# Moving x loads and output stores to ScalarE's queue, and finishing the last units chunk by chunk, in a four-layer graph network kernel

## The chip, the cores and the metric

The kernel runs on one core of one Trainium2 chip. The metric is device time in microseconds (us) of that core. A core has TensorE (PE; PEld is its weight load), VectorE (DVE), ScalarE (ACT), GpSimd (POOL) and SyncE (SP), each with its own instruction queue, worked off in order; they wait for each other by semaphores. DMAs are issued from SP's or ScalarE's queue ("SPq", "ACTq" in the profile) and then run by themselves. Instructions are known in the profile by the line of the kernel that issued them (L876).

## The reference, cut to what matters

x is 64 graphs of 256 nodes with 128 features; adj is one 256x256 adjacency matrix for all. Four layers follow each other, each `x = layernorm(x + layer(x))`, all in fp32:

```python
def _layernorm(x, axis=-1, eps=1e-5):
    m = jnp.mean(x, axis=axis, keepdims=True)
    v = jnp.var(x, axis=axis, keepdims=True)
    return (x - m) / jnp.sqrt(v + eps)

# layer 0: attention whose logits are sums over pairs of nodes, in an index pattern that depends on n alone
h = x @ others_weight
u1 = h @ att_weight[:f_out, 0]; u2 = h @ att_weight[f_out:, 0]
e = u1[:, idx1] + u2[:, idx2]
e = jnp.where(e >= 0, e, 0.1 * e)
att = softmax(jnp.where(adj > 0, e, NEG_BIG), axis=1)
out = jnp.einsum('bik,bkl->bil', att, h) + x @ self_weight
# layer 1: graph attention: softmax over leaky_relu(e_src + e_dst), masked by adj + I, then elu(attn @ (x @ W))
# layer 2: five steps of a gated recurrence: m = adj @ h; z, r = sigmoid(...); hv = tanh(...); h = (1-z)h + z hv
# layer 3: x W0 + sum over k = 1..3 of adj^k x (Wk + Wk+3)
```

## The kernel before, in words

Two graphs make a unit (UB = 2), so there are 32 units (NU) of 512 rows. Ten units are in flight, each in a lane (LANES) with its own SBUF buffers: unit u lives in lane u % 10, and when it ends, unit u + 10 starts there. The buffer `m` of a lane receives a unit's x from DRAM, and is used again for products later; `x` holds the unit's current features, and the output is stored from it.

The kernel does not issue instructions as it goes. Functions `layer0` to `layer3` record tasks with `add(engine, ns, fn, reads, writes)`: an engine, an estimated duration, a closure and the cells that it reads and writes. `Plan.run` then walks a simulated clock: for each engine that is free it takes the ready task with the lowest key. The key (`first`) is the unit's number times PERIOD plus the task's due time, which is reached by adding up estimated durations along the unit's own dependencies, times PACE (PACE_GATED in layer 2). The order in which tasks are taken is the order of each engine's instructions; semaphores are placed by dependency. A DMA recorded for SP occupies that queue for its estimate (540 ns for a load of x), and counts as landed 4 us later. PSUM has eight banks, taken by tasks when they start.

Names and lines that matter here:
- `load_x` (L301): for the first XDIRECT = 9 units, one DMA brings x with rows on partitions, and TensorE turns it (`feature_major`, L524, four transposes). For later units, four DMAs (L309) bring 32x32 blocks, and VectorE turns them (L626).
- Row sums in layer 0: for units from DIRECT_ROWS = 4 on, a vector `cu` is stored to DRAM (`to_row`, L551) and read back in another layout, both spread over all partitions (`from_row`, L555) and as 64x15 pieces (L655), which a small add (L658) sums to `d`. For units 0 to 3, TensorE spreads it by transposing a broadcast column (L567) and makes `d` by four 128x1 products (L664).
- Layer 1 (L735): units below HALVES = 2 go through attention graph by graph (two halves), others in one piece: Prelu (L741), Exp (L744), the multiply by the mask (L745), products with x (L752) and with W (L764).
- `warm` (L346): matmuls whose results nobody uses. Four stand at the start; six are recorded with the rank of a unit after the last, so that they are taken when TensorE has nothing else to do.
- Layer 2: `far(u, step)` says whether the features are turned by way of DRAM (L916, L919, L922) or on TensorE (L941). Each step has six 128x512 products on TensorE (L876), three tanh on ScalarE (L887, L895, L904) and four elementwise rows on VectorE.
- Layer 3: products with the weights (L977), copies (L981), products with adj squared (L984) into two banks, one for each chunk c of 128 nodes, then `layernorm` with the statistics (L578), `ve` (L580), `rstd` by pow on GpSimd (L583), the shift (L589, L591) and the normalized rows (L604 on ScalarE or L612 on VectorE).
- The output: for units below 29, one store on SP (L989). The last three units store each chunk by itself on SP (L993), chunk 0 normalized on VectorE and chunk 1 on ScalarE.

```python
        return (t.unit if t.unit < NU - LANES else NU - 1 - LATE - (NU - 1 - t.unit) * TAIL) * PERIOD + t.due
```

The functions that the diff touches, with the line numbers of the profile:

Of the kernel before, what the change touches and what calls it, by code (L numbers as in the profile page):

```python
# [9 lines left out]
AF = mybir.ActivationFunctionType  # L10
# [13 lines left out]
SCALES = True  # L24
SMALL = ("ve", "cu", "d", "elu", "shift")
TIGHT = 4
HALVES = 2
FIRST_FAR = {0: 2, 1: 2}
LAST_FAR = {0: 1}
PERIOD = 43e3  # L30
TAIL = 0.3
LATE = 6
PACE = 2.8
PACE_GATED = 1.56
HOLD = 80
DIRECT_ROWS = 4
XDIRECT = 9
START = 35e3
R2 = 1
R3 = 1.5  # L40
# [158 lines left out]
def kernel(  # L199
# [45 lines left out]
    def cell(name, shape):  # L245
        return Cell(sb(name, shape))
# [54 lines left out]
    def load_x(u, by="sp"):  # L301
        z = lanes[u % LANES]["m"]
        if u < XDIRECT:
            queue = {"sp": nc.sync, ACT: nc.scalar}[by]
            add(by, 600, lambda: queue.dma_start(z.ap.rearrange("p (b c d) -> p b c d", b=UB, c=NC), x_u[u]), (), (z,), dma=True, wait=800)
            return
        parts = object()
        for a in range(D // BL):
            add("sp", 540, lambda a=a: nc.sync.dma_start(  # L309
                z.ap[a * BL : (a + 1) * BL].rearrange("j (b i) -> j b i", i=BL),  # L310
                x_a[u, a].rearrange("(b j) i -> j b i", j=BL)), (), (z,), group=parts)

    w1 = load("w1", W, [D, D])
    load_x(0, ACT)
# [27 lines left out]
    def warm(n, after=()):  # L342

        for _ in range(n):
            ps = bank()
            add(PE, mm_ns(N), lambda ps=ps: nc.tensor.matmul(  # L346
                ps.ap[:, 0:N].rearrange("p (k n) -> p k n", k=2), ident.ap,
                ident.ap.rearrange("p (o n) -> p o n", o=1).to_broadcast([P, 2, P]), start=True, stop=True), (ident,), (ps,), after)
# [219 lines left out]
                ps.ap[:, g * P : (g + 1) * P], view()[:, g : g + 1].to_broadcast([P, P]), ident.ap), (src, ident), (ps,))  # L568
        return ps, lambda: ps.ap.rearrange("q (b c p) -> q b c p", b=UB, c=NC)

    def layernorm(u, L, pairs, swap=False, centred=False, last=False):

        st, ve, rstd, nm = L["st"], L["ve"], L["rstd"], L["nm"]
        sts, xs = object(), object()
        for k, (c, view) in enumerate(pairs):
            add(DVE, 330, lambda k=k, view=view: nc.vector.bn_stats(st.ap[:, k, :], view().rearrange("p j d -> p d j")),  # L578
                (c,), (st,), group=sts)
        small(u, "ve", 150, lambda eng: eng.tensor_scalar(  # L580
            ve.ap.rearrange("p (k j) -> p k j", k=2), st.ap.rearrange("p k (j s) -> p k j s", j=2)[:, :, :, 2], 1.0 / D, EPS,
            op0=ALU.mult, op1=ALU.add), (st,), (ve,))
        add(POOL, 1050, lambda: nc.gpsimd.tensor_tensor(rstd.ap, ve.ap, nhalf.ap, op=ALU.pow), (ve, nhalf), (rstd,))  # L583
        by_act = u >= TIGHT and plan.layer in NORM

        if by_act and not centred:
            mean = st.ap.rearrange("p k (j s) -> p k j s", j=2)[:, :, :, 1]
            if "shift" in SMALL:
                add(POOL, 280, lambda: nc.gpsimd.tensor_scalar_mul(  # L589
                    nm.ap.rearrange("p (k j) -> p k j", k=2), mean, -1.0), (st,), (nm,))  # L590
                add(POOL, 250, lambda: nc.gpsimd.tensor_mul(ve.ap, nm.ap, rstd.ap), (nm, rstd), (ve,))  # L591
            else:
                add(DVE, 120, lambda: nc.vector.scalar_tensor_tensor(
                    ve.ap.rearrange("p (k j) -> p k j", k=2), mean, -1.0,
                    rstd.ap.rearrange("p (k j) -> p k j", k=2), op0=ALU.mult, op1=ALU.mult), (st, rstd), (ve,))
        for k, (c, view) in enumerate(pairs):

            act = by_act and (k or not last)
            for j in range(2):
                b, ch = (j, k) if swap else (k, j)  # L600
                at = slice(2 * k + j, 2 * k + j + 1)
                shift, col = (ones, slice(0, 1)) if centred else (ve, at)
                if act:
                    add(ACT, 400, lambda j=j, b=b, ch=ch, view=view, at=at, shift=shift, col=col: nc.scalar.activation(  # L604
                        X[u].ap[:, b, ch, :], view()[:, j, :], AF.Identity, bias=shift.ap[:, col], scale=rstd.ap[:, at]),
                        (c, shift, rstd), (X[u],), group=xs)
                elif centred:
                    add(DVE, 260, lambda j=j, b=b, ch=ch, view=view, at=at: nc.vector.tensor_scalar(
                        X[u].ap[:, b, ch, :], view()[:, j, :], rstd.ap[:, at], 1.0, op0=ALU.mult, op1=ALU.add),
                        (c, rstd), (X[u],), group=xs)  # L610
                else:
                    add(DVE, 260, lambda k=k, j=j, b=b, ch=ch, view=view, at=at: nc.vector.tensor_scalar(  # L612
                        X[u].ap[:, b, ch, :], view()[:, j, :], st.ap[:, k, 3 * j + 1 : 3 * j + 2], rstd.ap[:, at],
                        op0=ALU.subtract, op1=ALU.mult), (c, st, rstd), (X[u],), group=xs)

    def y_pairs(y):
        v = y.ap.rearrange("p (b c d) -> p b c d", b=UB, c=NC)
# [3 lines left out]
    def layer0(u, L):  # L621
# [24 lines left out]
        small(u, "lrelu", 100, lambda eng: eng.scalar_tensor_tensor(  # L646
            cu.ap[:, 2], cu.ap[:, 2], 0.1, cu.ap[:, 2], op0=ALU.mult, op1=ALU.max), (cu,), (cu,))
        row, rv = on_all(u, lc, L["row"], cu, lambda: cu.ap[:, 2])
        if u >= DIRECT_ROWS:
            to_row(L["rowu"], cu, lambda: cu.ap[:, 0:2].rearrange("p k g -> p (k g)"), 2 * G)  # L650


            parts = object()
            for c in range(NC):
                add("sp", 560, lambda c=c: nc.sync.dma_start(  # L655
                    u4.ap[c * P // 2 : (c + 1) * P // 2],
                    L["rowu"].ap[:, c : c + 2 * T].rearrange("o (i n) -> (o i) n", n=16)[:, 0:15]), (L["rowu"],), (u4,), group=parts)
            small(u, "d", 100, lambda eng: eng.tensor_add(d.ap, u4.ap[:, 0:3:2], u4.ap[:, 12:15:2]), (u4,), (d,))  # L658
            ds = d
        else:  # L660
            ds = bank()
            for b in range(UB):
                for k in range(2):
                    add(PE, 240, lambda b=b, k=k: nc.tensor.matmul(  # L664
                        ds.ap[:, b : b + 1], xb[:, b, k : N : 2], wx0.ap[:, D + 2 + k : D + 3 + k],
                        start=(k == 0), stop=(k == 1)), (xT, wx0), (ds,))
# [61 lines left out]
    def layer1(u, L):  # L728
# [47 lines left out]
                        (ps_o, rs), (hp,), group=parts)  # L776
        if not u:
            plan.rank = NU
            warm(6, [plan.tasks[-1]])
            plan.rank = None  # L780

        sign = -1.0 if "elu" in SMALL and u >= TIGHT else 1.0
# [173 lines left out]
    def layer3(u, L):  # L956
        xT = turned(u, L, STEPS)
        aT, s = L["m"], L["z"]
        if STEPS in FAST and far(u, STEPS):
            left_fast(X[u], lambda g: X[u].ap.rearrange("p b c d -> p (b c) d")[:, g], adjf, L["r"], L["z"], aT)  # L960
            tail = [t for t in plan.tasks[-4:-3]]
        else:
            ps_a = bank()
            for b in range(UB):
                left(ps_a, X[u], b)
            add(ACT, 500, lambda: nc.scalar.copy(aT.ap, ps_a.ap), (ps_a,), (aT,))
            tail = list(ps_a.writers)

        ps = [bank() for _ in range(NC)]

        def view(c):
            return ps[c].ap.rearrange("p (k b d) -> p k b d", k=2, b=UB)

        for k, src in enumerate((xT, aT)):
            for c in range(NC):
                for b in range(UB):
                    add(PE, mm_ns(N), lambda k=k, src=src, c=c, b=b: nc.tensor.matmul(  # L977
                        view(c)[:, :, b, :], bn(src.ap)[:, b, c * P : (c + 1) * P], w3.ap[:, k],
                        start=(k == 0 and b == 0), stop=(k == 1), skip_group_check=True), (src, w3), (ps[c],), tail)
        for c in range(NC):  # L980
            add(ACT, 300, lambda c=c: nc.scalar.copy(s.ap[:, c * N : (c + 1) * N], ps[c].ap[:, N : 2 * N]), (ps[c],), (s,), group=ps)  # L981
        for c in range(NC):
            for mc in range(NC):
                add(PE, mm_ns(N), lambda c=c, mc=mc: nc.tensor.matmul(  # L984
                    ps[c].ap[:, 0:N], a2T.ap[:, mc, c * P : (c + 1) * P], s.ap[:, mc * N : (mc + 1) * N],
                    start=False, stop=(mc == NC - 1), skip_group_check=True), (a2T, s), (ps[c],))
        layernorm(u, L, [(ps[c], lambda c=c: view(c)[:, 0]) for c in range(NC)], swap=True, last=u >= NU - 3)
        if u < NU - 3:
            add("sp", 450, lambda: nc.sync.dma_start(out_u[u], X[u].ap), (X[u],), ())  # L989
            return  # L990

        for c, done in enumerate((plan.tasks[-4:-2], plan.tasks[-2:])):
            add("sp", 450, lambda c=c: nc.sync.dma_start(out_u[u][:, :, c], X[u].ap[:, :, c]), (), (), done)  # L993

    def spawn(u, lane):
        for k, layer in enumerate((layer0, layer1, layer2, layer3)):
# [47 lines left out]
```

The softmax here doesn't subtract the row's maximum and nothing guards it: scores larger than these inputs give would overflow.

## Time and profile before

| | |
|---|---|
| three runs, median (lowest to highest) | 1395.87 us (1395.82 to 1396.42) |
| span of the profiled execution | 1395.9 us, clock 0.999 |
| DVE busy | 1207.8 us, 2880 instructions |
| ACT busy | 936.3 us, 2155 instructions |
| POOL busy | 258.6 us, 492 instructions |
| DMA | 146.52 MB, 16 engines 46.7% busy for queue q1 (SP's), 0.1% for q10 (ScalarE's) |
| x loads and output stores on SP | 100 and 35 issues |

Busy time is the sum of the records of an engine; issuing a DMA is not counted in it. Records of matmuls overlap each other, and the page says that their ends are modelled. The slices divide the span into 40 equal parts; a digit is the busy share in tenths, and PEclk is the clock that TensorE was granted. A line of the waits reads: engine, what it was to write, its line, what it waited for, then total us, times, longest us. A line of a chain reads: start, us, engine, what is written, line.

### The profile page before, as it was taken

The page shows a single profiled execution, that of the slowest core. Times are in us where ns is not written, and L with a number is a line of the kernel's source. Part 1 is how long each engine was busy: PE and PEld are TensorE (multiplying, and loading weights), DVE is VectorE, ACT ScalarE, POOL GpSimd, SP SyncE. Part 2 cuts the span into 40 slices and gives each one's busy share as a digit, 9 for nine tenths or more (in the row PEclk, how much of TensorE's full clock was granted, in tenths as well). Part 3 has the DMA queues.
Part 4 walks back from the last instruction along what each step waited for, and adds up shares of the span by engine and source line. Part 5 has one row for each costly group of instructions (what it writes and reads, how often), then busy time and mean ns, then how long its engine had stood idle before and what let it go on. Part 6 is the DMA issues. An engine that isn't in the chain of part 4 may idle for free.

```text
span 1395.9 us, 21958 instructions
## 1 busy us (share of the span) xinstructions
PE 1387.0 (99%) x6549; PEld 965.9 (69%) x6549; DVE 1207.8 (87%) x2880; ACT 936.3 (67%) x2155; POOL 258.6 (19%) x492
## 2 busy tenths in 40 slices
PE   9999999999999999999999999999999999999998
PEld 8766666676666776676766767777666656666776
DVE  7898998998889888888899798899888998898953
ACT  5897754556676677667677688897765545665443
POOL 3211110021122112122111122132011100112222
PEclk9999999999999999999999999999999999999999
DMA  4223545365364555555554555545463453445521
GB/s 118 41 54 84 123 100 112 90 131 120 91 134 107 110 119 102 121 113 111 112 115 106 119 120 105 119 107 119 105 132 93 105 116 87 114 103 113 126 56 46
DMA packets 530791, 146.52 MB, mean 105 GB/s; under 512 B 457968, under 2 KB 496112, under 8 KB 530672
## 3 DMA queue, kind: packets, MB, share of 16 engines
q1 hardware_dynamic: 529872, 144.59, 46.7%
q8 instruction: 53, 0.87, 0.3%
q14 instruction: 66, 0.54, 0.2%
q10 hardware_dynamic: 800, 0.52, 0.1%
HBM read 80.57 MB, written 64.45 MB: 104 GB/s over the span
## 4 chain that ended last, share of the span: by engine, by line
PE 98%; DVE 1%; POOL 0%; ACT 0%; issue 0%; ACTq 0%; DVEq 0%; POOLq 0%
PE ps L876 49%; PE ps L819 17%; PE ps L977 8%; PE ps L802 5%; PE ps L715 4%; PE ps L984 4%; PE ps L752 4%; PE ps L764 2%; PE ps L710 2%; PE ps L639 2%; PE ps L346 0%; PE ps L524 0%; POOL rstd L583 0%; PE ps L941 0%; DVE st L578 0%; PE ps L567 0%
## 5 line engine op out<-in xcount | busy, mean ns | idle before, releaser
L876 PE MATMUL ps<-m,gT 128*128 128x512 f32 x960 | 464.3, 592 | 0.0
L876 PEld LDWEIGHTS ps<-m,gT 128*128 128x128 f32 x960 | 171.5, 190 | 119.9 <-issue 97.7
L895 ACT ACTIVATE e<-ps,bias 128x512 f32<-128x512 f32 x160 | 109.9, 687 | 120.2 <-PE ps L876 115.2
L887 ACT ACTIVATE e<-ps,bias 128x512 f32<-128x512 f32 x160 | 110.0, 687 | 91.7 <-PE ps L876 91.1
L583 POOL TENSOR_TENSOR rstd<-ve,nhalf 128x4 f32<-128x4 f32 x128 | 147.8, 1155 | 110.5 <-DVE ve L580 76.4
L876 PE MATMUL ps<-e,u5T 128*128 128x512 f32 x320 | 163.1, 592 | 0.0
L580 POOL TENSOR_SCALAR ve<-st 128x4 f32<-128x4 f32 x112 | 34.9, 311 | 691.1 <-DVE st L578 613.1
L819 PEld LDWEIGHTS ps<-adjTf,ht 128*128 128x128 f32 x726 | 115.7, 191 | 67.5 <-issue 57.1
L904 ACT ACTIVATE p<-ps,bias 128x512 f32<-128x512 f32 x160 | 109.6, 685 | 49.7 <-PE ps L876 45.9
L819 PE MATMUL ps<-adjTf,e 128*128 128x128 f32 x968 | 137.7, 275 | 0.0
L819 PEld LDWEIGHTS ps<-adjTf,e 128*128 128x128 f32 x968 | 125.2, 192 | 13.4 <-issue 12.4
L819 PE MATMUL ps<-adjTf,ht 128*128 128x128 f32 x726 | 122.4, 274 | 0.0
L906 DVE SCALAR_TENSOR_TENSOR p<-e,p 128x512 f32<-128x512 f32 x160 | 109.1, 683 | 11.1 <-ACT p L904 10.1
L876 PEld LDWEIGHTS ps<-e,u5T 128*128 128x128 f32 x320 | 59.9, 190 | 61.0 <-issue 46.8
L876 PE MATMUL ps<-xT,gT 128*128 128x512 f32 x192 | 96.7, 593 | 0.0
L846 DVE TENSOR_TENSOR m<-ps,e 128x256 f32<-128x256 f32 x152 | 63.0, 417 | 34.5 <-PE ps L819 28.9
L741 ACT ACTIVATE e<-m,esd 128x256 f32<-128x256 f32 x112 | 80.8, 765 | 0.0
L890 DVE SCALAR_TENSOR_TENSOR e<-e,xT 128x512 f32<-128x512 f32 x96 | 65.3, 680 | 13.6 <-ACT e L887 12.2
L537 DVE STREAM_TRANSPOSE p<-x 128x512 f32<-128x512 f32 x61 | 67.1, 1102 | 8.5 <-ACT x L604 7.4
L578 DVE BATCH_NORM_STATS2 st<-ps 128x6 f32<-128x256 f32 x128 | 51.5, 420 | 25.6 <-PE ps L984 18.2
L715 PEld LDWEIGHTS ps<-ht,p 128*128 128x128 f32 x512 | 66.0, 190 | 9.1 <-issue 7.9
L849 DVE TENSOR_TENSOR m<-ps,m 128x256 f32<-128x256 f32 x152 | 62.5, 415 | 9.5 <-PE ps L819 8.6
(187 smaller groups left out, 2864.4 us busy)
## 6 DMA issues: line engine op xcount, KB each, us to landing
hb<-p SPq DMA_DIRECT2D x182, 256.0 KB, 2.1
ht<-hb SPq DMA_DIRECT2D x484, 64.0 KB, 2.5
xT<-hb SPq DMA_DIRECT2D x244, 64.0 KB, 2.6
m<-row SPq DMA_DIRECT2D x56, 256.0 KB, 3.9
hb<-p SPq DMA_DIRECT2D x124, 64.0 KB, 1.8
ht<-hb SPq DMA_DIRECT2D x31, 256.0 KB, 3.0
out_dram<-x SPq DMA_DIRECT2D x29, 256.0 KB, 2.8
m<-in_x_dram SPq DMA_DIRECT2D x92, 64.0 KB, 2.3
```

Source lines behind the costliest of these rows:

```text
L537: add(DVE, 1050, lambda: nc.vector.transpose(v.ap.rearrange("p (a g i) -> p g a i", g=G, i=BL), X[u].ap.rearrange("p b c (j a) -> p (b c) ...
L583: add(POOL, 1050, lambda: nc.gpsimd.tensor_tensor(rstd.ap, ve.ap, nhalf.ap, op=ALU.pow), (ve, nhalf), (rstd,))
L715: add(PE, mm_ns(D + 2), lambda b=b, ic=ic, kc=kc, yv=yv: nc.tensor.matmul(yv()[:, ic, :], p.ap[:, b * NC + kc, ic * P : (ic + 1) * P], h.a ...
L741: add(ACT, 600, lambda g=g, b=b: nc.scalar.activation(e.ap[:, g, :].rearrange("p (c n) -> p c n", c=NC), ev()[:, b], AF.Prelu, bias=esd.ap ...
L802: add(PE, mm_ns(N), lambda b=b, mc=mc: nc.tensor.matmul(ps.ap[:, b * N : (b + 1) * N], lhs(b, mc), mat.ap[:, mc, :], start=(mc == 0), stop ...
L819: add(PE, mm_ns(P) + 4, lambda: nc.tensor.matmul(ps.ap[:, at * P : (at + 1) * P], lhs(), mat.ap[:, k, c * P : (c + 1) * P], start=True, st ...
L876: add(PE, mm_ns(T), lambda: nc.tensor.matmul(ps.ap, w(), rhs.ap, start=start, stop=stop, skip_group_check=True), (c, rhs), (ps,), after)
L887: add(ACT, 600, lambda ps_g=ps_g, up=up: nc.scalar.activation(r.ap, ps_g.ap, AF.Tanh, bias=bias2.ap[:, 1:2], scale=0.5 / up), (ps_g, bias2 ...
L895: add(ACT, 600, lambda ps_g=ps_g, up=up: nc.scalar.activation(z.ap, ps_g.ap, AF.Tanh, bias=bias2.ap[:, 0:1], scale=0.5 / up), (ps_g, bias2 ...
L904: add(ACT, 600, lambda ps_v=ps_v, up=up: nc.scalar.activation(v.ap, ps_v.ap, AF.Tanh, bias=bias2.ap[:, 2:3], scale=1 / up), (ps_v, bias2), ...
L906: add(DVE, 600, lambda: nc.vector.scalar_tensor_tensor(v.ap, z.ap, 1.0, v.ap, op0=ALU.add, op1=ALU.mult), (v, z), (v,))
L977: add(PE, mm_ns(N), lambda k=k, src=src, c=c, b=b: nc.tensor.matmul(view(c)[:, :, b, :], bn(src.ap)[:, b, c * P : (c + 1) * P], w3.ap[:, k ...
```

## The change

x loads from unit 10 on, and the output stores but those of the last two units, are recorded for ScalarE and issued from its queue. The last two units go through a new `layernorm_last`: each chunk has its own statistics, `ve` (on VectorE), pow (on GpSimd, 128x2 instead of 128x4) and shift (on VectorE); graph 1's rows of each chunk are normalized on ScalarE, graph 0's on VectorE, and each chunk is stored by SP as soon as its two rows are done. Unit 29 takes the ordinary way. The fourth unit (u = 3) makes its `d` by way of DRAM (DIRECT_D = 3), while its row is still spread by TensorE. XDIRECT goes from 9 to 10, so that unit 9's x is loaded by one DMA and turned by TensorE. HALVES goes from 2 to 0: no unit goes graph by graph through layer 1. PACE goes from 2.8 to 3.0.

```diff
--- before.py
+++ after.py
@@ -24,17 +24,19 @@
 SCALES = True
 SMALL = ("ve", "cu", "d", "elu", "shift")
 TIGHT = 4
-HALVES = 2
+HALVES = 0
+DIRECT_D = 3
+WARM = 6
 FIRST_FAR = {0: 2, 1: 2}
 LAST_FAR = {0: 1}
 PERIOD = 43e3
 TAIL = 0.3
 LATE = 6
-PACE = 2.8
+PACE = 3.0
 PACE_GATED = 1.56
 HOLD = 80
 DIRECT_ROWS = 4
-XDIRECT = 9
+XDIRECT = 10
 START = 35e3
 R2 = 1
 R3 = 1.5
@@ -306,9 +308,9 @@
             return
         parts = object()
         for a in range(D // BL):
-            add("sp", 540, lambda a=a: nc.sync.dma_start(
+            add(ACT, 540, lambda a=a: nc.scalar.dma_start(
                 z.ap[a * BL : (a + 1) * BL].rearrange("j (b i) -> j b i", i=BL),
-                x_a[u, a].rearrange("(b j) i -> j b i", j=BL)), (), (z,), group=parts)
+                x_a[u, a].rearrange("(b j) i -> j b i", j=BL)), (), (z,), group=parts, dma=True)
 
     w1 = load("w1", W, [D, D])
     load_x(0, ACT)
@@ -568,7 +570,7 @@
                 ps.ap[:, g * P : (g + 1) * P], view()[:, g : g + 1].to_broadcast([P, P]), ident.ap), (src, ident), (ps,))
         return ps, lambda: ps.ap.rearrange("q (b c p) -> q b c p", b=UB, c=NC)
 
-    def layernorm(u, L, pairs, swap=False, centred=False, last=False):
+    def layernorm(u, L, pairs, swap=False, centred=False):
 
 
 
@@ -594,13 +596,11 @@
                     ve.ap.rearrange("p (k j) -> p k j", k=2), mean, -1.0,
                     rstd.ap.rearrange("p (k j) -> p k j", k=2), op0=ALU.mult, op1=ALU.mult), (st, rstd), (ve,))
         for k, (c, view) in enumerate(pairs):
-
-            act = by_act and (k or not last)
             for j in range(2):
                 b, ch = (j, k) if swap else (k, j)
                 at = slice(2 * k + j, 2 * k + j + 1)
                 shift, col = (ones, slice(0, 1)) if centred else (ve, at)
-                if act:
+                if by_act:
                     add(ACT, 400, lambda j=j, b=b, ch=ch, view=view, at=at, shift=shift, col=col: nc.scalar.activation(
                         X[u].ap[:, b, ch, :], view()[:, j, :], AF.Identity, bias=shift.ap[:, col], scale=rstd.ap[:, at]),
                         (c, shift, rstd), (X[u],), group=xs)
@@ -612,6 +612,27 @@
                     add(DVE, 260, lambda k=k, j=j, b=b, ch=ch, view=view, at=at: nc.vector.tensor_scalar(
                         X[u].ap[:, b, ch, :], view()[:, j, :], st.ap[:, k, 3 * j + 1 : 3 * j + 2], rstd.ap[:, at],
                         op0=ALU.subtract, op1=ALU.mult), (c, st, rstd), (X[u],), group=xs)
+
+    def layernorm_last(u, pairs):
+
+        xs = object()
+        for k, (c, view) in enumerate(pairs):
+            st, ve, rstd = (cell(f"{name}{k}_{u}", [P, n]) for name, n in (("st", 6), ("ve", 2), ("rstd", 2)))
+            mean, var = (st.ap.rearrange("p (j s) -> p j s", j=2)[:, :, s] for s in (1, 2))
+            add(DVE, 330, lambda view=view, st=st: nc.vector.bn_stats(st.ap, view().rearrange("p j d -> p d j")), (c,), (st,))
+            add(DVE, 100, lambda ve=ve, var=var: nc.vector.tensor_scalar(
+                ve.ap, var, 1.0 / D, EPS, op0=ALU.mult, op1=ALU.add), (st,), (ve,))
+            add(POOL, 1050, lambda ve=ve, rstd=rstd: nc.gpsimd.tensor_tensor(rstd.ap, ve.ap, nhalf.ap[:, 0:2], op=ALU.pow),
+                (ve, nhalf), (rstd,))
+            add(DVE, 100, lambda ve=ve, mean=mean, rstd=rstd: nc.vector.scalar_tensor_tensor(
+                ve.ap, mean, -1.0, rstd.ap, op0=ALU.mult, op1=ALU.mult), (st, rstd), (ve,))
+            done = [add(ACT, 400, lambda k=k, view=view, ve=ve, rstd=rstd: nc.scalar.activation(
+                X[u].ap[:, 1, k, :], view()[:, 1, :], AF.Identity, bias=ve.ap[:, 1:2], scale=rstd.ap[:, 1:2]),
+                (c, ve, rstd), (X[u],), group=xs),
+                add(DVE, 260, lambda k=k, view=view, mean=mean, rstd=rstd: nc.vector.tensor_scalar(
+                    X[u].ap[:, 0, k, :], view()[:, 0, :], mean[:, 0:1], rstd.ap[:, 0:1], op0=ALU.subtract, op1=ALU.mult),
+                    (c, st, rstd), (X[u],), group=xs)]
+            add("sp", 450, lambda k=k: nc.sync.dma_start(out_u[u][:, :, k], X[u].ap[:, :, k]), (), (), done)
 
     def y_pairs(y):
         v = y.ap.rearrange("p (b c d) -> p b c d", b=UB, c=NC)
@@ -646,7 +667,7 @@
         small(u, "lrelu", 100, lambda eng: eng.scalar_tensor_tensor(
             cu.ap[:, 2], cu.ap[:, 2], 0.1, cu.ap[:, 2], op0=ALU.mult, op1=ALU.max), (cu,), (cu,))
         row, rv = on_all(u, lc, L["row"], cu, lambda: cu.ap[:, 2])
-        if u >= DIRECT_ROWS:
+        if u >= DIRECT_D:
             to_row(L["rowu"], cu, lambda: cu.ap[:, 0:2].rearrange("p k g -> p (k g)"), 2 * G)
 
 
@@ -776,7 +797,7 @@
                         (ps_o, rs), (hp,), group=parts)
         if not u:
             plan.rank = NU
-            warm(6, [plan.tasks[-1]])
+            warm(WARM, [plan.tasks[-1]])
             plan.rank = None
 
         sign = -1.0 if "elu" in SMALL and u >= TIGHT else 1.0
@@ -984,13 +1005,12 @@
                 add(PE, mm_ns(N), lambda c=c, mc=mc: nc.tensor.matmul(
                     ps[c].ap[:, 0:N], a2T.ap[:, mc, c * P : (c + 1) * P], s.ap[:, mc * N : (mc + 1) * N],
                     start=False, stop=(mc == NC - 1), skip_group_check=True), (a2T, s), (ps[c],))
-        layernorm(u, L, [(ps[c], lambda c=c: view(c)[:, 0]) for c in range(NC)], swap=True, last=u >= NU - 3)
-        if u < NU - 3:
-            add("sp", 450, lambda: nc.sync.dma_start(out_u[u], X[u].ap), (X[u],), ())
+        pairs = [(ps[c], lambda c=c: view(c)[:, 0]) for c in range(NC)]
+        if u >= NU - 2:
+            layernorm_last(u, pairs)
             return
-
-        for c, done in enumerate((plan.tasks[-4:-2], plan.tasks[-2:])):
-            add("sp", 450, lambda c=c: nc.sync.dma_start(out_u[u][:, :, c], X[u].ap[:, :, c]), (), (), done)
+        layernorm(u, L, pairs, swap=True)
+        add(ACT, 450, lambda: nc.scalar.dma_start(out_u[u], X[u].ap), (X[u],), (), dma=True)
 
     def spawn(u, lane):
         for k, layer in enumerate((layer0, layer1, layer2, layer3)):
```

## The prediction

> **What bounds the kernel now.** I read the page first (busy time, slices), then what TensorE waited for, then the chain of work at both ends, then the DMA issues. The page:
>
> ```profile
> span 1395.9 us, 21958 instructions
> PE 1387.0 (99%) x6549; PEld 965.9 (69%) x6549; DVE 1207.8 (87%) x2880; ACT 936.3 (67%) x2155; POOL 258.6 (19%) x492
> PE   9999999999999999999999999999999999999998
> PEclk9999999999999999999999999999999999999999
> ```
>
> A full PE row may hide gaps, because a matmul's record is longer than its turn (592 ns for 128x512, while the starts of consecutive ones lie 429 ns apart). So I checked it in two ways. All waits that TensorE's matmuls had in the whole run are these:
>
> ```profile
> PE ps L346 <- POOL ident masks.py:199: 1.3, 1, 1.3
> PE ps L977 <- DVE m L846: 0.4, 1, 0.4
> PE ps L664 <- ACT ht L642: 0.3, 1, 0.3
> ```
>
> And summing start-to-start intervals in the trace above the shortest ones of each shape (429 ns for 512 columns, 215 for 256, 111 for 128), the stretch from 60 to 1388 us holds about 5 us of excess, nearly all rounding of 1 to 3 ns a matmul; its only hole is 0.54 us at 297.2 us. From 25 us to the last matmul TensorE is full. What is not useful TensorE work lies at the ends: the first 1.3 us, warm-up products (L346) at the start, twelve more records of L346, fillers at the lowest rank, and the time after the last matmul:
>
> ```profile
> 37.77 2.75 PE L346 MATMUL ps<-ident 128*128 128x256 f32 x12
> ```
>
> ```profile
> 1388.80 0.39 DVE st L578
> ...
> 1389.23 0.44 DVE st L578
> ...
> 1389.75 0.20 POOL ve L580
> ...
> 1390.03 0.23 POOL nm L589
> 1390.25 0.99 POOL rstd L583
> 1391.24 0.18 POOL ve L591
> ...
> 1391.60 0.65 ACTq L1039
> 1392.25 0.70 ACT x L604 x2
> ```
>
> This is the chain of waits behind the last matmul: statistics, four GpSimd steps, two ScalarE rows; then the last store, issued at 1393.09, and the end at 1395.9. From the last matmul's end (1389.16 us, when the second statistics are released) that is 6.7 us. So a change can gain only at the two ends and in TensorE's own work, a few us together; it can lose anywhere, by making TensorE wait.
>
> **What the Trainium skill says.** "DMA: Bandwidth & Descriptors", section "Issuing engines are not separate DMA queues": DMAs begun by different engines run on the same 16 engines, and spreading them saves only the sequencer's time. The trace agrees in that almost all bytes were one queue's (144.59 of 146.52 MB) while the DMA share was 46.7%. "Perfetto Trace Analysis", section "DMA Instruction — HWDGE (DVE, Sync)": the issuing sequencer is held until the descriptors are made, and may wait for a lock on a generator shared by two sequencers. The trace shows the holding (an x load's issue takes 487 ns in the median), and hardly the lock: at 0.72 us SP and ScalarE issued at once and took 394 and 453 ns, like issues made alone.
>
> **The change part by part.**
>
> *Queues.* 22 units' x loads, four issues each, and 30 output stores go from SP to ScalarE. The rows that carry the price:
>
> ```profile
> L989 SPq DMA_DIRECT2D out_dram<-x x29: 378/400/573, 188.8 to 1379.8; - x29
> L309 SPq DMA_DIRECT2D m<-in_x_dram x92: 312/487/1295, 13.4 to 1180.7; - x92
> ```
>
> 88 x 0.483 (mean) + 30 x 0.42 = 55 us more on ScalarE's queue, and about as much less on SP's, which issues 1413 DMAs in 769 us. ScalarE goes from 936 us busy to some 990 of 1395, 71%. On SP nothing is gained on the path: no matmul waited for a DMA. On ScalarE a load is a block of about 1.95 us, and behind it stand tanh, exponentials and copies of other units on which matmuls depend. Against that stands the slack: matching the 160 products of u5T by r with the VectorE row (L890) that feeds each, in the order of the instruction list, the product begins 0.42 us after it at least, 2.26 in the median, under 2 us in 74 cases. The order is also made anew: the plan charges each issue 540 ns (loads) or 450 (stores), a little more than measured, and puts the instructions behind it later. A load's wait for the old readers of `m` stalls ScalarE too now; SP waited 29.1 us in 17 such waits for L977, but SP stood there with nothing else to do. I take 0.3 us for all of it; bounds -0.5 (the hole at 297 us goes, as it hangs on an order that is made anew) and +15 us (22 loads that each cost TensorE the 0.7 us by which a block exceeds the tightest tenth of the slacks, 1.2 us).
>
> *Fourth unit's row sums.* Four 128x1 products (L664) go: 8 records at 0.100 us (3.2 us of intervals over 32) = -0.80 us of TensorE. In their place one store and two loads on SP, and a small VectorE add that waits for them: the vector is ready at 26.3 us, 1.5 us to land in DRAM, two issues of 0.57 and 3.1 us to land back give 32.5 us, and VectorE reaches that add near 36 us. Hidden.
>
> *Tenth unit's x (XDIRECT 10).* One load instead of four, and four transposes on TensorE instead of one on VectorE: 4 x 0.109 = +0.44 us of TensorE.
>
> *No halves, pace 3.0.* Same matmuls, other order. Unit 0's attention multiply is now one 128x1024 instruction (about 1.2 us) before its four products, and unit 1's stands ahead of unit 0's layer-1 end on VectorE. By the durations of before, in the new VectorE order: unit 1's multiply from 36.3 to 37.5 us, two 512-wide steps to 38.7, statistics to 39.5, then four rows of units 2 and 3 (0.7 + 0.6 + 0.35 + 0.68) to 41.9, and unit 0's x complete at 43.0 instead of 40.2 us. TensorE's order fills this: before unit 0's transposes it now has unit 1's products with p (1.73 us) and by W (0.90), and of unit 2 four (0.89) and seven (1.57) products that came later before, together 5.09 us, and lacks 1.80 us (units 7 and 9, L639). So when TensorE reaches unit 0 at 43.0 instead of 40.36, it has 5.09 - 1.80 = 3.29 us more behind it: 43.0 - 40.36 - 3.29 = -0.65 us, in which the -0.80 and +0.44 above are contained. No view shows these waits, so bounds of -1.5 and +1.0; I take -0.5, having found two later places up to 60 us where the result comes less than 0.3 us before its product.
>
> *Last units chunk by chunk.* Before, the last unit's pow handles 128x4 after both statistics, ve, nm. Now each chunk has its own: statistics, a VectorE ve, pow on 128x2, a VectorE shift, and one row each on ScalarE and VectorE. Four pows instead of two stand in GpSimd's order, the first free 1.35 us before the last matmul's end. pow on 128x2 is not in the trace: 128x4 takes 1.03 us alone, other GpSimd operations of this width 0.19, so if the rest scales with elements 0.19 + 0.42 = 0.61; at worst still 1.03. With 0.61 the last pow waits for its ve (1.3 us after the last matmul, behind unit 31's row on VectorE) and ends at 1.9, ScalarE's last row at 2.75, against 3.79 before: -1.0 us. With 1.03 the four pows queue to 2.8, the row ends at 3.5: -0.3. The store behind it stays (2.9 us to the end). I take -1.0, as no row at hand says that the time is fixed. Unit 29 loses its chunked store, which isn't last.
>
> Sum: -0.5 - 1.0 + 0.3 - 0.4 (most of the 0.54 us hole) = -1.6 us against the span of 1395.9, which the three runs bear out (median 1395.87): 1394.3 us.
>
> **Rivals.** *ScalarE's queue becomes the wait (slower).* A block of four issues, 1.95 us, with SP issuing 55% of the time beside it, lands before a tanh whose product has less slack. If half of the 22 loads cost TensorE 0.6 us each, that is +6.6 us, net about 1401; it decides from 0.2 us a load (22 x 0.2 = 4.4 us, which eats the gain and 2.8 more). For it: 74 slacks under 2 us, VectorE at 87% which cannot catch up fast. Against: ScalarE idles a third, and the order is made with these costs in it.
> *The ends give more.* If the new order also finds work for the 2.6 us of fillers' place, and the hole goes, the early part gives 1.5 to 2 us and the tail 1.3: 1392.4 us. For it: the fillers are pure loss. Against: in the new order all six still stand together before unit 1's products, so TensorE is again without work there.
> *The tail's change does nothing*, since four pows at full price replace two and the early order only breaks even: 1395.6 us.
>
> **How the numbers follow.** A run of this kernel can tell about 0.2%, 2.8 us, from no change. The forecast has a chance of 0.60, 1393.0 to 1396 with a tip of 0.05 beyond -2.8 us; more at the ends 0.15 (1391.5 to 1393); the flat tail 0.07; ScalarE's waits 0.18, of which 0.03 stay within 2.8 us. So faster 0.20, same 0.65, slower 0.15. The range 1392.0 to 1399.0 leaves the far part of the two outer cases out.
>
> **What would show it.** TensorE's waits stay under 1 us each with a sum under 3 us; ScalarE's queue shows 88 and 30 issues of 0.4 to 0.5 us; fillers end near 38 us; unit 0's transposes near 43; rstd on 128x2 near 0.6 us; the last store 2.9 us before the end, about 5.7 us from the last matmul. Wrong if TensorE waits repeatedly for ScalarE or for VectorE rows fed by it within a few us of x loads, if issues on ScalarE take over 0.7 us, or if the middle's period of 42.4 us per unit changes.

## The result, and the profile after

The changed kernel is slower: 1415.22 us (median of 4 runs, 1412.5 to 1416.63) against 1396.14 us for the kernel before on the same chip, ratio 1.0133 [1.0116, 1.0151]. The forecast was 1394.3 us with a range up to 1399.0. The profiled execution spans 1410.7 us at clock 0.999; traces are compared by their own spans (1395.9 before). It is the fastest of the four executions; the other three span 1413.0 to 1414.8 us at granted clocks of 0.997 and 0.998, so the traces show 14.8 us of loss where the medians show 18.6.

The page, with the lines that answer those of before:

```profile
span 1410.7 us, 21942 instructions
PE 1390.8 (99%) x6545; PEld 966.0 (68%) x6545; DVE 1205.2 (85%) x2884; ACT 936.1 (66%) x2154; POOL 265.9 (19%) x488
PE   9999999999999999999999999999999999999998
PEclk9999999999999999999999999999999999999999
...
q1 hardware_dynamic: 466272, 130.96, 41.3%
q10 hardware_dynamic: 63104, 14.16, 4.7%
```

Nothing here shows the loss: busy times stand nearly as they were, and the slices of PE are full to the last tenth. It is in what TensorE's matmuls waited for (the first five of eleven lines):

```profile
PE ps L840 <- ACT e L852: 5.2, 5, 2.9
PE ps L897 <- DVE m L873: 2.2, 3, 1.1
PE ps L897 <- ACT e L908: 1.7, 1, 1.7
PE ps L348 <- POOL ident masks.py:199: 1.3, 1, 1.3
PE ps L998 <- ACT e L916: 0.9, 1, 0.9
```

Before there were three such lines, and only the ident was over 0.4 us. Now ScalarE's copies and tanh (L852, L908, L916) come late. And what came ahead of them, in the chain of waits at one such place (start, us, what):

```profile
659.73 3.92 DMA ht<-hb
663.64 0.02 issue
663.67 0.32 ACTq L311
663.98 0.05 issue
664.03 0.70 ACT e L916
664.73 0.02 issue
664.75 0.69 DVE p L923
```

This chain is the finding. An x load on ScalarE (L311) is released by the landing of `ht<-hb`, a transfer of SP's for another unit, which shares no data with it. ScalarE works in order, so a tanh stands behind the load, VectorE's rows behind the tanh, and TensorE loses 1.4 us in three holes up to 673 us. At another place the load waits for its own kind; the timeline there (start, us, engine, line; in brackets the idle time ahead and its releaser):

```profile
743.43 5.12 SPq L545 DMA_DIRECT2D xT<-hb  x4
...
743.68 5.17 ACTq L311 DMA_DIRECT2D m<-in_x_dram  x3
...
748.90 0.69 ACT L908 ACTIVATE e<-ps,bias 128x512 f32<-128x512 f32 x1 [4.85 <-DMA m<-in_x_dram]
748.95 0.44 ACTq L311 DMA_DIRECT2D m<-in_x_dram  x1
749.49 0.26 ACT L852 COPY e<-ps 128x128 f32<-128x128 f32 x1
...
749.80 0.49 PE L840 MATMUL ps<-adjTf,e 128*128 128x128 f32 x2 [2.91 <-ACT e L852]
```

Three of a unit's four issues take 5.17 us, because the third stands until the first, which raises the same semaphore, has landed, and TensorE is empty for 2.9 us.

The records of the instructions say why. Each DMA raises one of eight semaphores, and SP and ScalarE draw on the same eight: in both kernels, every one of them is used 176 or 177 times, whichever engine issues. 86 of the 118 moved issues carry in the instruction a wait for the very semaphore that they are to raise. Summed over the trace, ScalarE stood 27.9 us ahead of the 118 issues, 27 us of it at loads, longest 3.98 us; where the last DMA with that semaphore was SP's 15.6 us, where it was ScalarE's own 12.4 us. Comparing start-to-start intervals of matmuls as the prediction did, the last matmul starts at 1404.29 instead of 1388.74 us; the stretch from 60 to 1388 us, 5 us of excess before, now holds 20.

### The profile page after: what moved, and what is told of

Its sections match the earlier page's. It is cut to its first block, busy times and chain, and to the rows that moved or that the text cites. A ratio compares the mean times of both kernels' runs of the same rounds, so it can differ in the third digit from the quotient of the medians.

```text
span 1410.7 us, 21942 instructions
## 1 busy us (share of the span) xinstructions
PE 1390.8 (99%) x6545; PEld 966.0 (68%) x6545; DVE 1205.2 (85%) x2884; ACT 936.1 (66%) x2154; POOL 265.9 (19%) x488
## 4 chain that ended last, share of the span: by engine, by line
PE 91%; DVE 3%; DMA 2%; ACT 2%; issue 1%; POOL 0%; SPq 0%; ACTq 0%; DVEq 0%; POOLq 0%
PE ps L897 46%; PE ps L840 15%; PE ps L998 7%; PE ps L823 5%; PE ps L736 4%; PE ps L1005 4%; PE ps L773 3%; PE ps L731 2%; PE ps L785 2%; PE ps L660 2%; DMA m<-in_x_dram 1%; DMA xT<-hb 0%; DMA m<-row 0%; ACT e L762 0%; DMA ht<-hb 0%
## 5 line engine op out<-in xcount | busy, mean ns | idle before, releaser
L916 ACT ACTIVATE e<-ps,bias 128x512 f32<-128x512 f32 x160 | 109.9, 687 | 101.4 <-PE ps L897 96.1
L908 ACT ACTIVATE e<-ps,bias 128x512 f32<-128x512 f32 x160 | 109.8, 687 | 100.9 <-PE ps L897 82.3
L709 ACT ACTIVATE p<-e,nm 128x256 f32<-128x256 f32 x128 | 63.8, 504 | 15.9 <-DVE nm L707 10.6
L852 ACT COPY e<-ps 128x128 f32<-128x128 f32 x152 | 40.2, 265 | 50.4 <-PE ps L840 38.0
```

The lines of the kernel that those rows point to most:

```text
L709: add(ACT, 400, lambda g=g: nc.scalar.activation(p.ap[:, g, :], e.ap[:, g, :], AF.Exp, bias=nm.ap[:, g : g + 1], accum_out=s.ap[:, g : g + ...
L908: add(ACT, 600, lambda ps_g=ps_g, up=up: nc.scalar.activation(r.ap, ps_g.ap, AF.Tanh, bias=bias2.ap[:, 1:2], scale=0.5 / up), (ps_g, bias2 ...
L916: add(ACT, 600, lambda ps_g=ps_g, up=up: nc.scalar.activation(z.ap, ps_g.ap, AF.Tanh, bias=bias2.ap[:, 0:1], scale=0.5 / up), (ps_g, bias2 ...
```

## The experiments

Times against the kernel before are (ratio - 1) x 1397 us, with "+" for slower; the changed kernel stands at +18.6. The theories T1 to T5 are named in the first expectation.

**Which part: the queue alone, all but the queue.** First the changed kernel with both edits of the queue undone:

```diff
-            add(ACT, 540, lambda a=a: nc.scalar.dma_start(
+            add("sp", 540, lambda a=a: nc.sync.dma_start(
...
-        add(ACT, 450, lambda: nc.scalar.dma_start(out_u[u], X[u].ap), (X[u],), (), dma=True)
+        add("sp", 450, lambda: nc.sync.dma_start(out_u[u], X[u].ap), (X[u],), ())
```

> The changed kernel with its x loads and output stores issued by SP again; all else of the change stays. Theories. T1: a load's instruction on ScalarE stands until an earlier DMA that carries the same semaphore (mostly one of SP's) has landed, and ScalarE's tanh and copies stand behind it; SP has no such work behind it. T2: the time of issuing itself, 88 x 0.42 + 30 x 0.40 = 49 us on ScalarE, pushes its work back. T3: the other edits (pace 3.0, no halves, chunked last units, fourth unit by DRAM) cost the time. T4: the load waits on ScalarE for the last reader of m. T5: two queues issuing at once slow each other. Expected: T1, T2, T4, T5 about 1394 to 1396 (before is 1396.1); T3 about 1410 to 1415.

Measured 1397.99 us, ratio 1.0009 [1.0001, 1.0017]: +1.3, some 2 us above what T1 expected, which the runs on the pace below take up. Then the reverse, the kernel before with only these two edits made:

> The kernel before with one edit of the change alone: x loads of units 10 and up, and the output stores, issued by ScalarE. T1, T2, T4, T5: about 1410 to 1416, as slow as the changed kernel. T3 (the other edits cost the time): about 1396.

Measured 1414.50, ratio 1.0127 [1.0112, 1.0143]: +17.7. The queue carries the loss. (4.2 us of this kernel's stand at 6.6 us: with XDIRECT 9, unit 9's four loads now stand on ScalarE ahead of the copy of adj.) The stores and the loads each alone:

> The changed kernel with its x loads issued by SP again and the output stores left on ScalarE. T1: 1395 to 1397, since in the changed kernel's trace nearly all of ScalarE's idle time ahead of a DMA stands at the loads. T2: 30 of 118 issues stay, so a quarter of the loss, about 1400. T3: about 1410 to 1415.

> The changed kernel with its output stores issued by SP again and the x loads left on ScalarE; with the stores alone moved it took 1401.3, with neither 1398.0, with both 1415.2. T1 (a load stands on ScalarE until an earlier DMA with its semaphore has landed): 1409 to 1414, nearly all of the loss, and the idle time of ScalarE ahead of the loads stays at 20 us or more. If loss went by the number of issues (T2): three quarters of it, 1398 + 0.75 x 17.2 = 1411, so this run alone doesn't part the two; what parts them is where the holes of PE stand: T1 behind loads that waited, T2 spread.

Stores alone 1401.31, ratio 1.0032 [1.0019, 1.0044]; loads alone 1413.05, ratio 1.0113 [1.0100, 1.0127], with 28 us of idle time ahead of the loads. So the loads carry most. The stores, at no cost by T1, came 3.2 us above the kernel with both on SP, near what T2 expected (about 1400); the runs with copies below speak against T2. One cause is seen in that trace, and it runs the other way (chain of waits, stores alone):

```profile
283.81 2.79 DMA out_dram<-x
286.60 0.02 issue
286.62 0.34 SPq L557
```

SP's load of a row waits for ScalarE's store to land, as they share a semaphore. How much of the 3.2 us is this, and how much the new order, these runs don't part.

**Issue time or wait for readers.** Loads and stores on SP, and a ScalarE copy of unused data in place of each, which has the same dependencies in the plan:

```diff
+    def idle_work(k, ns, deps):
+        flat = wk.ap.rearrange("p a b -> p (a b)")
+        add(ACT, ns, lambda: nc.scalar.copy(flat[:, 512:896], flat[:, 0:384]), (wk,), (), deps)
...
+            idle_work(a, 540, t.deps)
```

> Loads and stores issued by SP, and in place of each on ScalarE a copy of 128x384 unused elements (about 0.4 us each, 118 of them, as long as the issues) that waits for the same work as the load or the store does, at the same price in the plan. T2 (issue time) and T4 (the wait for the last reader of m): about 1410 to 1416, as slow as the changed kernel. T1 and T5: 1394 to 1397.

Measured 1399.05, ratio 1.0017 [1.0010, 1.0023], 1.1 us above the kernel without the copies, though they took 0.51 us each, 60 us of ScalarE's time. So issue time (T2) does not cost the 17. T4 this run does not test: the dependencies put a copy behind the readers of `m` in the order, but the instruction touches other data, and in the trace none of the 118 copies carries a wait for another engine. The records of the changed kernel settle T4: of its 88 loads on ScalarE, 86 carry a wait for a DMA's semaphore, two carry none, and none carries one for TensorE or VectorE. (On SP, in the kernel before, 21 of 92 carried one for TensorE.)

**How much is the order.** The planner makes the order anew from each edit. The two ends of the change alone (`layernorm_last`, DIRECT_D = 3) on the kernel before show what that can do:

> The kernel before with only the two ends of the change: last two units chunk by chunk, fourth unit's row sums by DRAM; queues, pace, halves and the tenth unit's load as before. The steps of the prediction for these give -0.8 (row sums) and -1.0 (tail): 1394.9 against 1396.7. If the order that the planner makes from it opens holes as it did in the kernel with all on SP: 1397 to 1398.

Measured 1401.93, ratio 1.0033 [1.0021, 1.0046]: +4.6 where -1.8 was expected, with holes up to 1.5 us that no DMA on ScalarE explains. So the times of two kernels with different orders can't be compared here to better than some 6 us. The next three therefore keep the changed kernel's order exactly (TensorE's and VectorE's lists of instructions are identical), and change only what the closures issue (the stores likewise go to SP):

```diff
-            add(ACT, 540, lambda a=a: nc.scalar.dma_start(
+            add(ACT, 540, lambda a=a: nc.sync.dma_start(
```

> The changed kernel with the planner's order untouched (each load and store keeps its place in the plan as ScalarE's task, so PE, VectorE and ScalarE's other work stand in the same order), and only the queue that issues them is SP's. It takes away what an order made anew by the planner can do by itself (the runs so far: the same work in other orders 1395.8 to 1401.9). If the queue alone costs the time (T1 waits on ScalarE, T2 issue time, T5 two queues): 1395 to 1399. If the order made for ScalarE's queue is at fault: 1410 or more.

```diff
+    def idle_work():
+        flat = wk.ap.rearrange("p a b -> p (a b)")
+        nc.scalar.copy(flat[:, 512:896], flat[:, 0:384])
...
+                idle_work()
```

> As the kernel before it in this call, in the same order, and ScalarE does a copy of 128x384 unused elements (about 0.4 us) at each of the 118 places where it issued a load or a store. T2 (issue time, 49 us in all): 1410 or more. T1 and T5: within 1.5 us of the kernel without the copies.

```diff
+    def wait_for(part):
+        flat = wk.ap.rearrange("p a b -> p (a b)")
+        nc.scalar.copy(flat[BL : 2 * BL, 512:513], part)
...
+                if a == 3:
+                    wait_for(z.ap[BL : 2 * BL, 0:1])
```

> As the first kernel of this call, in the same order, all DMAs by SP, but after each unit's fourth load ScalarE copies 32x1 elements that the unit's second load brings, so that it waits for a landing, 22 times. Nothing is issued by ScalarE. T1 (ScalarE waiting for a DMA's landing is the cost): with some 1.3 us of waiting 22 times, about the 28 us of the changed kernel, slower by 8 to 18 us, 1404 to 1416. T2 and T5: within 1.5 us of the kernel without it.

Measured: SP in this order 1401.67, ratio 1.0034 [1.0021, 1.0047]; with the copies 1402.32, 1.0038 [1.0025, 1.0050]; with the waits 1409.54, 1.0086 [1.0073, 1.0100]. The first was a miss upwards: the kernel with the order made for ScalarE's queue is 4.7 us slower than before with no DMA of its loads or stores on ScalarE. But in the same order ScalarE's queue costs 13.8 us more (12.0 between the two traces), 118 copies (60 us of ScalarE's time) 0.6, and 22 waits for a landing, with nothing issued by ScalarE, 7.3, just under the expected 8 to 18. At the place of the timeline above, the kernel with SP in the same order reads:

```profile
737.33 0.34 SPq L311 DMA_DIRECT2D m<-in_x_dram  x1
...
738.26 0.42 SPq L311 DMA_DIRECT2D m<-in_x_dram  x1
...
739.06 0.69 ACT L908 ACTIVATE e<-ps,bias 128x512 f32<-128x512 f32 x1 [1.35 <-PE ps L897]
739.64 0.26 ACT L852 COPY e<-ps 128x128 f32<-128x128 f32 x1
```

The same tanh waits for its own product, and the hole is gone. Hole by hole, 9.5 us of the 12.0 us by which the two traces' last matmuls differ are nine holes of the changed kernel that this one lacks, at 227, 622 to 623, 667 to 673, 747, 793 and 1053 us, each within 10 us behind a load that waited. Holes at 343, 355, 924, 1112 and 1254 us stand in both: they are the order's.

**Length of a wait, second queue, pace.** The wait put in by hand cost less for each us waited than the changed kernel's. So a longer wait was tried (for the fourth load's landing instead of the second's):

```diff
-                    wait_for(z.ap[BL : 2 * BL, 0:1])
+                    wait_for(z.ap[3 * BL : 4 * BL, 0:1])
```

> As the kernel in which ScalarE waits for the landing of each unit's second load (1409.5; 45.9 us waited in 21 waits for a loss of 7.9 us against the same order without it), but it waits for the fourth load, which it reaches right after that load is issued. T1 with some slack before PE misses the tile (the prediction found a median of 2.3 us): each wait is some 1.2 us longer, 22 x 1.2 = 26 us more waited, and past the slack nearly all of it is lost: 1420 to 1436. If waited time costs in proportion (0.17 us of loss for each us): 1413 to 1416.

Measured 1451.68, ratio 1.0388 [1.0360, 1.0415]. The two kernels' waits (us in total, times, longest), the shorter first:

```profile
ACT wk L305 <- DMA m<-in_x_dram: 45.9, 21, 3.9
```

```profile
ACT wk L305 <- DMA m<-in_x_dram: 91.9, 22, 5.8
```

Waits of 2.2 us in the mean cost 7.3 us together, waits of 4.2 us cost 49.5 (ratio 1.0388 against 1.0034), so the second 46 us of waiting cost 42. Not all of this is waiting. The trace of the longer wait has four stretches of 3.41 us before its last matmul in which TensorE was granted half its clock, each within 2 us behind holes of 2.6 us or more together; the trace of the shorter wait has none. One of them, and the stretch behind another hole of 2.9 us that has none (window, its length, busy us of PE, PEld, DVE, ACT and POOL with their instructions; then PEclk, DMA share, GB/s):

```profile
193.20:196.60 3.40, 3.40 (x9) 2.18 (x8) 2.57 (x9) 0.89 (x3) 1.11 (x1) 0.50 0.31 77
467.10:470.50 3.40, 3.38 (x12) 2.39 (x13) 2.50 (x5) 3.40 (x8) 0.00 (x0) 1.00 0.02 7
```

By start-to-start intervals the matmuls lost 6.5 us in the four stretches. Some 35 of the 42 us are left: beyond the first 2 us about three quarters of a wait is lost, an estimate from these two kernels. The time came above the expected 1420 to 1436, since the wait grew by 2 us each and not 1.2, and since the clock was not thought of.

Next the loads from a third queue, in the changed kernel's order:

```diff
-            add(ACT, 540, lambda a=a: nc.scalar.dma_start(
+            add(ACT, 540, lambda a=a: nc.gpsimd.dma_start(
```

> The changed kernel in its own order, with the loads issued by GpSimd and the stores by SP. T5 (loads from a second queue beside SP's slow each other's transfers): as slow as the changed kernel, 1411 to 1416. T1: 1400 to 1404, as in the same order with all on SP (1401.7).

GpSimd's loads raise eight semaphores of their own (11 uses each in the trace). Measured 1404.62, ratio 1.0058 [1.0043, 1.0073]: 3.4 us above SP's queue in the same order, 10.5 below ScalarE's, and just over T1's range of 1400 to 1404. So there is little room for T5, a second queue that slows the transfers. With the loads recorded as GpSimd's tasks of 1000 ns, so that the order is made for it, and stores on SP:

> The changed kernel with the x loads issued by GpSimd, and the stores by SP. T1: 1396 to 1399, as with both on SP: no ScalarE instruction stands behind a load, whatever the load waits for. T5 (a second queue that issues beside SP's slows the transfers): slower than with both on SP by several us, 1402 or more. Bound of GpSimd's own cost: it is busy 19% of the span, and 88 issues of 1 us would make it 25%.

Measured 1400.39, ratio 1.0024 [1.0015, 1.0034]: just over T1's 1396 to 1399 and short of T5's 1402, 2.1 us above all on SP. Loads land later from there (median 3.0 us against 2.4).

Last, the pace, with ScalarE's queue, then SP's in the same order, then SP's in its own:

```diff
-PACE = 3.0
+PACE = 2.8
```

> The changed kernel, loads and stores on ScalarE, with the pace at 2.8 as in the kernel before; with both on SP this pace gave 1395.8 against 1398.0 at pace 3.0. If the pace and the queue act each for itself: 1415.2 - 2.2 = 1413. If the loss needs the later pace: under 1402.

> The order that the planner makes at pace 2.8 for ScalarE's queue (1404.0 with the DMAs issued by ScalarE), with the queue SP's. T1: the waits go and the order's own price stays: 1396 to 1399. If the order alone makes the 1404.0: 1402 to 1405.

> Loads and stores on SP, all else of the change, but the pace at 2.8 as in the kernel before. The kernel with pace 3.0 took 1398.0, before 1396.7: the ends should give 1.5 us but the middle holds about 2 us of holes (335.3, 749.7, 880.5, 1238.4 us) that the kernel before hasn't. If the pace makes these: 1395 to 1396. If the tenth unit's load in one piece or the missing halves make them: 1397.5 to 1398.5.

Pace 2.8 with ScalarE's queue: 1404.00, ratio 1.0049 [1.0036, 1.0063], between both expectations. Its order with SP's queue: 1398.85, 1.0015 [1.0008, 1.0022]; so at this pace the queue in an unchanged order costs 4.7 us and not 13.8 (ScalarE stood 18 us ahead of its DMAs, longest 3.1). All on SP at pace 2.8 in its own order: 1395.79, ratio 0.9990 [0.9981, 0.9998]. That is the best version, faster than both kernels, than the one before by 1.4 us. Its matmuls' waits:

```profile
PE ps L348 <- POOL ident masks.py:199: 1.3, 1, 1.3
PE ps L660 <- ACT ht L663: 0.3, 1, 0.3
PE ps L569 <- DVE cu L667: 0.2, 1, 0.2
```

The loss of 18.6 us, put together: edits other than queue and pace, in their own order, -1.4; pace 3.0 +2.6 (1.0009 against 0.9990); the order made for ScalarE's places +3.5 (1.0034 against 1.0009); issue time +0.6; what is left, +13.3, is what ScalarE's queue costs beyond issue time: the waits at its DMAs, with whatever SP's waits for ScalarE's DMAs add, which no run prices by itself.

How 27.9 us of waiting come to 13.3 is argued, not measured. At the price of the shorter wait put in by hand (45.9 us for 7.3) they would make 4.4. But ScalarE's waits are uneven: those within 7 us of each other add up to blocks of up to 4.6 us. Priced between the two hand-made waits they make some 8 us, an estimate. Another 2 us is the difference between the medians (13.8) and the traces (12.0), and goes with the lower clock of the executions that were not profiled. Some 3 us stay without a price.

## Why the prediction was wrong, point by point

**The step that failed** is the queue's price: "A load's wait for the old readers of `m` stalls ScalarE too now ... I take 0.3 us for all of it". It measured 13.8 us in an unchanged order. The wait for old readers was the wrong wait: in the changed kernel none of the 88 loads carries one. The wait that counts is for an earlier DMA's landing, through a shared semaphore, and the prediction has no term for it. It stood in the trace of the kernel before: 731 of SP's 1413 issues carry a wait for the semaphore that they raise, and the x loads landed 1.8 to 5.4 us after issue. I also read the price from a row that can't hold it. The Trainium skill says in "Perfetto Trace Analysis", section "DMA Instruction — HWDGE (DVE, Sync)", that the reported time of a DMA instruction starts when all its semaphores are satisfied. The trace agrees: the row

```profile
L311 ACTq DMA_DIRECT2D m<-in_x_dram x88: 317/352/1065, 187.4 to 1201.8; - x88
```

is no dearer than before (352 ns against 487 on SP), while ScalarE stood 27 us ahead of it.

*The slack* (2.26 us in the median) was right in kind: waits of 2.2 us cost a third of a us each, waits of 4.2 us 2.3 (2.0 without the loss at half clock). But I set it against a block of 1.95 us, and the blocks reached 5.2.

*Rival 1*, ScalarE's queue becomes the wait, had place and sign right; its 6.6 us were half of the 13.8. Its counter-argument, "the order is made with these costs in it", failed: the plan charges 540 ns for an issue and nothing for a wait on another DMA's semaphore. The sentence from the Trainium skill that the prediction leaned on ("DMA: Bandwidth & Descriptors", section "Issuing engines are not separate DMA queues": spreading saves only the sequencer's time) is not contradicted: no matmul waited for a DMA before, and no run here shows a gain from SP's 118 issues less.

*Order and pace.* "Same matmuls, other order", with bounds of -1.5 and +1.0 us, was too narrow: order and pace cost +3.5 and +2.6, and the ends alone, in a new order, went to +4.6.

*The edits at the ends* came near their steps, as the best version shows. Forecast: early part -0.5, hole -0.4, tail -1.0. There, by intervals up to the last matmul, the first 60 us gave -0.1, the middle -0.65 (the hole at 297 us is gone), the tail -0.65: together -1.4 of -1.9. In the changed kernel the tail reads:

```profile
1405.06 1.50 POOL L625 TENSOR_TENSOR rstd<-ve,nhalf 128x2 f32<-128x2 f32 x2 [0.37 <-DVE ve L623]
...
1405.82 1.82 ACT L629 ACTIVATE x<-ps,ve,rstd 128x128 f32<-128x128 f32 x4 [4.19 <-DVE ve L623]
...
1406.31 1.98 SPq L635 DMA_DIRECT2D out_dram<-x  x4
```

pow on 128x2 took 0.70 us (0.61 estimated), the last row ended 2.9 us after the last matmul (2.75), and the end came 6.4 us after that matmul's start instead of 7.1. The mis-sized terms are pow and the store: four issues of two units stand in a row on SP, and the last starts 0.2 us after its row is done.

*What would show it wrong* was named rightly: TensorE waiting repeatedly for ScalarE within a few us of x loads. That is what the trace shows.

**Open.** Why pace 3.0 makes the waits three times as dear as 2.8 is not settled; the sum of waits, 27.9 against 18 us, explains a part. (The trace of pace 2.8 with ScalarE's queue has one half-clock stretch, at 828 us, that cost 1.7 us; the changed kernel's has none before its last matmul.) Loads on ScalarE with semaphores of their own were not tried.

## What to carry to other kernels

Before moving a DMA to an engine that computes, ask what its issue waits for (a semaphore shared with other DMAs as much as a buffer), and put that wait, with landing times from the trace, against the slack behind the engine; the issue's own record doesn't hold it. SP, which does nothing else, waited in the kernel before without a matmul waiting for a DMA. A copy that stands in for a DMA tests a wait only if its own instruction carries that wait. And where an order is planned, test an edit inside an unchanged order first: here orders of nearly the same work spread over 6 us, with no load or store on ScalarE.

## What the runs showed of the hardware that I had not expected

The Trainium skill ("PSUM — Partial Sum Buffer", section "Engine vs sequencer instructions") says that ScalarE's queue is strictly first in, first out; the trace agrees, down to a DMA's semaphore holding up a tanh by 4.85 us. An issue of the same load took 0.35 us in the median on ScalarE, 0.48 to 0.49 on SP and 0.66 on GpSimd. The loss by waiting was far from proportional: twice the waiting cost 6.8 times as much (49.5 against 7.3 us), 6.5 us of it at half clock. Stretches of 3.41 us at half the granted clock also stand in the traces of the queue alone (12 us), loads alone (703 us) and pace 2.8 with ScalarE's queue (828 us), each within 2 us behind a hole of TensorE of 2.4 us or more. Not every such hole has one: in the profiled execution of the changed kernel the hole of 2.9 us at 747 us has none.
